# A two-layer graph network in fp32: the set-up's first norm split between two engines, and the output weight transposed earlier

## The chip, the core and the metric

The program runs on one core of a Trainium2 chip. A core has a matrix engine (TensorE; PE in the profile, with its weight loads shown apart as PEld), VectorE (DVE), ScalarE (ACT), GpSimd (POOL) and SyncE (SP), which here only issues transfers. Each engine works through its own queue of instructions in order and waits on semaphores for the others. TensorE reads from the on-chip memory SBUF and writes to PSUM; VectorE and ScalarE take results out of PSUM. Sixteen DMA engines move data between the chip's main memory and SBUF.

The metric is the device time of one execution in microseconds. The median of four runs of the kernel before is 3507.7 us (3506.65 to 3508.15).

## The reference, cut to what matters

The input x is 8 batches of 2048 tokens with 256 features, in fp32, and adj is a 2048 x 2048 adjacency matrix of integers. Each of two layers normalises its input, clamps it at zero, and adds the layer's result to x:

```
h = max(layernorm(x), 0)
x = x + L0(h, adj)          # attention with 4 heads of 64
h = max(layernorm(x), 0)
x = x + L1(h, adj)          # graph attention, one head
```

L0 is this, for each batch, with keys taken in chunks of 256 and a softmax within each chunk:

```
q, k, v = h @ Wq.T + bq, h @ Wk.T + bk, h @ Wv.T + bv
scores  = clip(q . k / 8, -10, 10);  scores = -10 where adj == 0
ctx     = sum over chunks of softmax(scores) @ v
out     = layernorm(ctx @ Wo.T + bo + h) * gamma + beta
```

The four weights Wq, Wk, Wv and Wo are 256 x 256 and enter transposed. L1 projects with another 256 x 256 matrix, builds attention weights from a source term and a target term, masks them by adj, and multiplies.

## The kernel before, in words

**Tiling.** Tokens are handled in blocks of 512 (four tiles of 128), four blocks to a batch. A block's normalised features `hn` (tokens on partitions) are transposed on TensorE into `hT` (features on partitions), from which queries, keys and values are projected. All matmuls are fp32.

**Stages.** A set-up of about 75 us transposes the weights, projects queries, keys and values of all four blocks of batch 0, and turns most of the adjacency matrix into an int8 tile `bound`. Then the batches follow each other. Each has 32 attention steps (`Attention.begin` and `Attention.end`, half a step each), into which other pieces are woven by a table of half-steps: `todo` in general, and `once` (L1153) for pieces that only batch 0 has. Between the attention of two batches stands the second layer.

**Order.** The whole order is written out by hand (`tc.manual_schedule`, L1029): each engine runs its instructions in the order of the source text. A transfer is issued by the queue of the engine that is named, nearly always `nc.sync`, in source order too.

**PSUM.** There are eight banks in three tags of two buffers: `s` (two banks each), `n` and `t`. During set-up `ps_m()` gives `n` and `t` in turn, so that every fourth call reuses a buffer and has to wait until that buffer was emptied; `ps_h()` takes `s`.

**The start of the set-up (L1036 to L1088).** SP issues the loads of block 0's x, of Wq, Wk and Wv (`load_weight`, L233), of three biases, of block 1's x, and of four pieces of adjacency (`load_rows`, L262). Meanwhile TensorE transposes the identity 16 times (`warm(16)`, L1054), which nobody reads. `stats`, `power` and `shift` (L402 to L411) compute block 0's mean and inverse deviation, `stats` and `shift` on VectorE, `power` as three small activations on ScalarE. `turn_weight` (L249) transposes one weight as four 128 x 128 squares into one PSUM tile and copies it out on VectorE; it is called for q, k and v, and eight more identity transposes follow. `norm` (L413, by `normed`, L374) has ScalarE normalise and clamp the four tiles of the block, `Relu(scale * x + bias)`, in two calls. `turn` (L416) transposes a half of the features, and VectorE copies half 0 into `hT`, ScalarE half 1. Then block 1's `stats`, `power` and `shift` are queued, two adjacency pieces are compared with zero (`find`, L1069, by `missing_of`, L271, on VectorE with a copy on GpSimd), and `qk` (L440) projects the queries and then the keys of block 0, each in two PSUM tiles of tag `s`, which ScalarE empties (L451).

**Buffers.** Raw weights and `hn` tiles share one tag of five buffers (`hn_tile`, L210). A tile is one [128, 2, 256] square, so a block takes two.

**The output weight.** It is loaded by `load_output_weight` (L238) as four transfers, because its columns are regrouped by head (runs of 32 values). That happens in half-step 1 of batch 0, after the set-up, and `turn_weight` on it in half-step 5. It is first used in half-step 24 (`output_tiled`, L726, eight half-steps into the second block).

Of the kernel before, what the change touches and what calls it, by code (L numbers as in the profile page):

```python
# [12 lines left out]
AF = mybir.ActivationFunctionType  # L13
ALU = mybir.AluOpType
# [14 lines left out]
def gnn_two_layers(  # L29
# [18 lines left out]
    nc = tc.nc  # L48
# [31 lines left out]
    def ps_m():  # L80
        if turn_about[0]:
            turn_about[1] += 1
            if turn_about[1] % 2:
                return ps_n()
        return ps_t()
# [20 lines left out]
    wqT = const.tile([P, FC, F], F32, name="wqT")  # L106
    wkT = const.tile([P, FC, F], F32, name="wkT")
    wvT = const.tile([P, FC, F], F32, name="wvT")
    woT = const.tile([P, FC, F], F32, name="woT")
# [56 lines left out]
    def in_key_order(queries):  # L166
        return queries.rearrange("p (t i b) -> p t i b", i=QUADS, b=Q)
# [13 lines left out]
    def store_bounds(part):  # L181
        nc.sync.dma_start(of_half(part), bounds[part])
# [16 lines left out]
    def column(src, name):  # L199
        t = const.tile([P, FC], F32, name=name)  # L200
        nc.sync.dma_start(t, src.rearrange("(c p) -> p c", p=P))
        return t
# [7 lines left out]
    def hn_tile(name="hn"):  # L210
        return work.tile([P, 2, F], F32, tag="hn", name=name, bufs=5)
# [6 lines left out]
    def pe(piece):  # L218

        piece.kind = "pe"  # L220
        return piece
# [11 lines left out]
    def load_weight(w):  # L233
        raw = hn_tile("raw")
        nc.sync.dma_start(raw, w.rearrange("(c p) f -> p c f", p=P))
        return raw

    def load_output_weight(w):  # L238

        raw = hn_tile("raw")  # L240
        for c in range(FC):
            of_heads = w[c * P:(c + 1) * P, :].rearrange("p (h k d) -> p h k d", h=HEADS, k=2)
            for k in range(2):
                nc.sync.dma_start(
                    raw[:, c, k * P:(k + 1) * P].rearrange("p (h d) -> p h d", h=HEADS), of_heads[:, :, k, :]
                )
        return raw

    def turn_weight(raw, wT):  # L249
        pt = ps_m()  # L250
        for di in range(FC):
            for do in range(FC):
                k = di * FC + do
                nc.tensor.transpose(pt[:, k * P:(k + 1) * P], raw[:, do, di * P:(di + 1) * P], ident)
        nc.vector.tensor_copy(wT.rearrange("p c f -> p (c f)"), pt)

    HALF = N // 2
    in_setup = [True]
# [106 lines left out]
    def norm_shift(engine, mv, rn):  # L365

        engine.tensor_tensor(rn[:, 1, :], rn[:, 1, :], mv[:, :, 0], op=ALU.mult)  # L367
# [16 lines left out]
    def transposed(hns, c):  # L384

        pt = ps_m()
        for t in range(TB):
            nc.tensor.transpose(pt[:, t * P:(t + 1) * P], hns[t // 2][:, t % 2, c * P:(c + 1) * P], ident)
        return pt


    class Projection:
# [16 lines left out]

        def shift(self, nb):  # L410
            norm_shift(self.adder, self.mv[nb], self.rn[nb])  # L411

        def norm(self, nb, t2):  # L413
            self.hns.setdefault(nb, []).append(normed(self.x[nb], self.rn[nb], t2))
# [621 lines left out]
    proj = Projection(0)  # L1036
    turn_about[0] = True
    raws = {}
    proj.load(0)
    for name, w in (("q", wq), ("k", wk), ("v", wv)):  # L1040
        raws[name] = load_weight(w)
    bq_c = column(bq, "bq_c")
    bk_c = column(bk, "bk_c")
    bv_r = row_bcast(bv, "bv_r")
# [4 lines left out]
    def warm(times):  # L1049
        pt = ps_m()  # L1050
        for k in range(times):
            nc.tensor.transpose(pt[:, k % TB * P:(k % TB + 1) * P], ident, ident)

    warm(16)  # L1054
    proj.stats(0, range(TB))
    proj.power(0)
    turn_weight(raws["q"], wqT)
    proj.shift(0)
    turn_weight(raws["k"], wkT)
    turn_weight(raws["v"], wvT)  # L1060
    warm(8)
    proj.norm(0, 0)
    proj.norm(0, 1)
    proj.load(2)
    proj.turn(0, 0)
    proj.turn(0, 1)
    proj.tiles()

    def find(*parts):  # L1069
# [18 lines left out]
    for nb in range(NNB - 1):  # L1088
        i = 6 * nb
# [52 lines left out]
    def layer1_vector(i):  # L1142
        a_r = work.tile([P, F], F32, tag="r", name="a_r")
        nc.sync.dma_start(a_r, row(a1[i * F:(i + 1) * F, 0]))
        prod = hn_tile("prod")
        for c in range(FC):
            nc.vector.scalar_tensor_tensor(
                prod[:, c, :], w1s[:, c, 0:F], 1.0, a_r, op0=ALU.mult, op1=ALU.mult,
                accum_out=w1s[:, c, F + i:F + i + 1],
            )  # L1150


    once = {  # L1153
        1: [lambda: raws.update(o=load_output_weight(wo)), layer1_weight],
        2: [lambda: [store_bounds(part) for part in HALVES_OF[:3]]],
        5: [pe(lambda: turn_weight(raws["o"], woT))],
        6: [lambda: layer1_vector(0)],
        7: [lambda: layer1_vector(1)],
        HALVES - PER: [find_lone],
# [305 lines left out]
```

## Time and profile before

| what | value |
|---|---|
| median of four runs | 3507.7 us |
| profiled execution | 3507.57 us |
| its span, first to last instruction | 3505.8 us |
| TensorE busy | 3496.7 us (100%) |
| VectorE, ScalarE, GpSimd busy | 75%, 56%, 52% |
| granted TensorE clock | 1.00 |
| DMA in the first fortieth of the span (88 us) | 247 GB/s, engines 70 to 80% busy |

A row of the timeline has the start in us, the duration in us, the engine, the line of the kernel, the operation, what it writes and reads (out<-in), the shape and how often it ran; in brackets stands the idle time of the engine before it and what ended it. SPq is the sequencer of SP issuing transfers. The chain that ended last is read backwards by the profiler from the last instruction, at each step to what released it; its rows have start, duration and the work. Matmul ends are modelled, so that a busy TensorE is not one at its peak.

### The profile page before, as it was taken

The page shows a single profiled execution, that of the slowest core. Times are in us where ns is not written, and L with a number is a line of the kernel's source. Part 1 is how long each engine was busy: PE and PEld are TensorE (multiplying, and loading weights), DVE is VectorE, ACT ScalarE, POOL GpSimd, SP SyncE. Part 2 cuts the span into 40 slices and gives each one's busy share as a digit, 9 for nine tenths or more (in the row PEclk, how much of TensorE's full clock was granted, in tenths as well). Part 3 has the DMA queues.
Part 4 walks back from the last instruction along what each step waited for, and adds up shares of the span by engine and source line. Part 5 has one row for each costly group of instructions (what it writes and reads, how often), then busy time and mean ns, then how long its engine had stood idle before and what let it go on. Part 6 is the DMA issues. An engine that isn't in the chain of part 4 may idle for free.

```text
span 3505.8 us, 104599 instructions
## 1 busy us (share of the span) xinstructions
PE 3496.7 (100%) x46076; PEld 2308.5 (66%) x46076; DVE 2632.3 (75%) x3983; ACT 1958.3 (56%) x2961; POOL 1824.6 (52%) x1198
## 2 busy tenths in 40 slices
PE   9999999999999999999999999999999999999999
PEld 5455775667765577566876758656686655864578
DVE  6887777877678676786767867678686785857876
ACT  6777426763267633676336763367623776147751
POOL 5677017870278702786037850378503784047841
PEclk9999999999999999999999999999999999999999
DMA  7545323443234531444314443244432335124331
GB/s 247 127 109 124 95 87 72 97 111 105 67 87 86 119 100 61 92 93 110 103 61 92 93 106 103 65 92 87 121 103 65 79 85 128 62 53 93 80 79 52
DMA packets 171320, 332.13 MB, mean 95 GB/s; under 512 B 28656, under 2 KB 90352, under 8 KB 170864
## 3 DMA queue, kind: packets, MB, share of 16 engines
q0 software_dynamic: 32832, 119.03, 18.6%
q1 hardware_dynamic: 129712, 205.36, 18.3%
q8 instruction: 360, 5.90, 0.7%
q10 hardware_dynamic: 8320, 1.05, 0.2%
q14 instruction: 96, 0.79, 0.1%
HBM read 156.50 MB, written 51.44 MB: 59 GB/s over the span
## 4 chain that ended last, share of the span: by engine, by line
PE 98%; DVE 1%; ACT 0%; DMA 0%; POOL 0%; issue 0%; ACTq 0%; DVEq 0%; POOLq 0%
PE ps_s L503 25%; PE ps_n L519 25%; PE ps_s L994 12%; PE ps_t L531 7%; PE ps_n L994 6%; PE ps_t L994 6%; PE ps_t L743 2%; PE ps_t L447 2%; PE ps_n L447 2%; PE ps_s L447 2%; PE ps_n L461 2%; PE ps_t L843 1%; PE ps_t L461 1%; PE ps_n L843 1%; PE ps_s L843 0%; PE ps_n L721 0%
## 5 line engine op out<-in xcount | busy, mean ns | idle before, releaser
L543 DVE SCALAR_TENSOR_TENSOR e<-ps_s,bound 128x1024 f32<-128x1024 f32 x1024 | 1219.0, 1221 | 400.4 <-PE ps_s L503 395.4
L558 POOL TENSOR_TENSOR both<-e 128x1024 f32<-128x1024 f32 x512 | 1221.7, 2417 | 542.4 <-PE ps_t L531 245.2
L503 PE MATMUL ps_s<-q,k 64*32 64x512 f32 x16384 | 1332.3, 590 | 0.1
L552 ACT ACTIVATE e<-e 128x1024 f32<-128x1024 f32 x1024 | 1049.1, 1049 | 456.2 <-DVE e L543 439.0
L519 PE MATMUL ps_n<-e,v 64*32 64x512 f32 x16384 | 1118.3, 589 | 0.0
L503 PEld LDWEIGHTS ps_s<-q,k 64*32 64x32 f32 x16384 | 504.3, 106 | 399.2 <-issue 277.9
L519 PEld LDWEIGHTS ps_n<-e,v 64*32 64x32 f32 x16384 | 523.8, 107 | 361.8 <-issue 266.5
L531 PE MATMUL ps_t<-both,ones 64*32 64x512 f32 x4096 | 548.1, 590 | 0.0
L994 PE MATMUL ps_s<-g,w 128*128 128x257 f32 x2048 | 448.5, 380 | 0.0
L994 PEld LDWEIGHTS ps_s<-g,w 128*128 128x128 f32 x2048 | 388.7, 190 | 55.7
L573 DVE TENSOR_TENSOR prod<-ps_n,rz 128x512 f32<-128x512 f32 x448 | 288.9, 687 | 135.9 <-ACT rz L564 86.5
L1017 POOL TENSOR_TENSOR x<-x,r 128x256 f32<-128x256 f32 x124 | 90.5, 744 | 457.1 <-ACT r L1015 456.3
L977 DVE SCALAR_TENSOR_TENSOR w<-bound,w 128x1024 f32<-128x1024 int8 x256 | 314.7, 1229 | 8.7
L367 POOL TENSOR_TENSOR krn<-krn,mv 128x4 f32<-128x4 f32 x28 | 6.7, 240 | 560.9 <-DVE w L971 560.9
L994 PE MATMUL ps_n<-g,w 128*128 128x257 f32 x1024 | 292.5, 382 | 0.0
L994 PE MATMUL ps_t<-g,w 128*128 128x257 f32 x1024 | 289.9, 380 | 0.0
L563 ACT ACTIVATE rz<-ps_t 128x512 f32<-128x512 f32 x256 | 152.4, 595 | 237.5 <-PE ps_t L531 164.2
L971 DVE TENSOR_SCALAR w<-src,cd 128x512 f32<-128x512 f32 x512 | 263.4, 557 | 17.7 <-ACT src L951 13.8
L578 POOL DMA_DIRECT2D ctxT<-prod x224 | 192.6, 860 | 56.5 <-DVE sd L852 50.2
L994 PEld LDWEIGHTS ps_n<-g,w 128*128 128x128 f32 x1024 | 193.0, 190 | 44.1 <-issue 17.6
L531 PEld LDWEIGHTS ps_t<-both,ones 64*32 64x32 f32 x4096 | 151.7, 106 | 101.9 <-SPq L475 44.1
L994 PEld LDWEIGHTS ps_t<-g,w 128*128 128x128 f32 x1024 | 194.0, 189 | 28.0
(139 smaller groups left out, 2974.0 us busy)
## 6 DMA issues: line engine op xcount, KB each, us to landing
ctxT<-prod POOLq DMA_DIRECT2D x224, 512.0 KB, 5.0
bound<-bound_d SPq DMA_DIRECT2D x125, 512.0 KB, 4.5
turned_d<-squares SPq DMA_DIRECT2D x232, 128.0 KB, 2.8
hT<-turned_d SPq DMA_DIRECT2D x58, 512.0 KB, 4.6
rows<-in_adj_dram SPq DMA_DIRECT2D x32, 512.0 KB, 5.0
x<-in_x_dram SPq DMA_DIRECT2D x32, 512.0 KB, 6.3
out_dram<-x SPq DMA_DIRECT2D x31, 512.0 KB, 2.7
xp<-in_x_dram SPq DMA_DIRECT2D x28, 512.0 KB, 4.5
```

Source lines behind the costliest of these rows:

```text
L447: nc.tensor.matmul(in_key_order(pp) if i == 0 else pp, w[:, di, do * P:(do + 1) * P], h, start=di == 0, stop=di == FC - 1,)
L503: nc.tensor.matmul(self.s[n, o][c * Q:(c + 1) * Q, kt, :], self.k[p][rows, at:at + Q], self.q[p][rows, nb * NB:(nb + 1) * NB], start=True, ...
L519: made.append(nc.tensor.matmul(self.num[n, c][h * Q:(h + 1) * Q, :], self.v[rows, j * KT + kt, at:at + Q], self.e[n, p][rows, i * KT + kt, :],
L531: nc.tensor.matmul(self.total[n][h * Q:(h + 1) * Q, :], ones[rows, :], self.both[n, h // 2][rows, h % 2, :], start=half == 1, stop=half == 0,)
L543: nc.vector.scalar_tensor_tensor(self.e[n, p][:, i * KT:(i + 1) * KT, :], self.s.pop((n, o)), -CLIP * SC, bounds[nb, j // 4][:, j % 4 * KT ...
L552: nc.scalar.activation(e, e, AF.Exp, scale=1.0 / SC)
L558: nc.gpsimd.tensor_tensor(self.both[n, p], e[:, 0], e[:, 1], op=ALU.add)
L573: nc.vector.tensor_tensor(dst[:, c, :], self.num.pop((n, c)), self.rz[n], op=ALU.mult)
L578: nc.gpsimd.dma_start(self.ctxT[nb], self.prod.pop(n), accum_op=ALU.add)
L971: nc.vector.tensor_scalar(w[:, i, :], self.src[nb], self.cd[:, 0, j:j + 1], self.cd[:, 1, j:j + 1], op0=ALU.mult, op1=ALU.max,)
L977: nc.vector.scalar_tensor_tensor(two, bounds1[nb, j // 8][:, j % 8 - 1:j % 8 + 1, :], 0.0, two, op0=ALU.is_gt, op1=ALU.mult)
L994: nc.tensor.matmul(accs[t][:, 0:F + 1], w[:, i, t * P:(t + 1) * P], g[:, j, :], start=j == 0, stop=j == NT - 1,)
```

## The change

Five edits, all in the set-up or in what it takes over from the loop:

1. The four loads of the output weight are issued right after those of Wq, Wk and Wv, ahead of the biases, of block 1's x and of the adjacency.
2. Its transposes stand behind those of q, k and v, in the place of the eight identity transposes. In the loop, half-steps 1 and 5 lose the load and the transposes.
3. Transposing a weight and taking it out of PSUM are two calls now. The copy of q stays where it was. That of k goes to ScalarE, behind its norms; those of v and o stay on VectorE and come behind the eviction of the block's first half.
4. Two of the block's four tiles are normalised by VectorE, without the clamp.
5. Both evictions of the transposed block clamp at zero, VectorE with a maximum, ScalarE with Relu. For the two tiles that ScalarE clamped already this changes nothing.

```
-    def turn_weight(raw, wT):
+    def turned_weight(raw):
         pt = ps_m()
...
-        nc.vector.tensor_copy(wT.rearrange("p c f -> p (c f)"), pt)
+        return pt
+
+    def keep_weight(pt, wT, engine):
+        dst = wT.rearrange("p c f -> p (c f)")
+        if engine is nc.vector:
+            nc.vector.tensor_copy(dst, pt)
+        else:
+            nc.scalar.activation(dst, pt, AF.Copy)
...
+        def norm_signed(self, nb, t2):
+            hn, rn = hn_tile(), self.rn[nb]
+            for i in range(2):
+                t = 2 * t2 + i
+                nc.vector.tensor_scalar(
+                    hn[:, i, :], self.x[nb][:, t, :], rn[:, 0, t:t + 1], rn[:, 1, t:t + 1], op0=ALU.mult, op1=ALU.add
+                )
+            self.hns.setdefault(nb, []).append(hn)
+
+        def turn_signed(self, nb, c):
+            if c == 0:
+                self.hT[nb] = Features()
+            pt = in_key_order(transposed(self.hns[nb], c))
+            if c == 0:
+                nc.vector.tensor_scalar(self.hT[nb].queries(0), pt, 0.0, None, op0=ALU.max)
+            else:
+                nc.scalar.activation(self.hT[nb].queries(c), pt, AF.Relu)
...
         raws[name] = load_weight(w)
+    raws["o"] = load_output_weight(wo)
...
-    turn_weight(raws["q"], wqT)
+    keep_weight(turned_weight(raws["q"]), wqT, nc.vector)
     proj.shift(0)
-    turn_weight(raws["k"], wkT)
-    turn_weight(raws["v"], wvT)
-    warm(8)
+    turned = {name: turned_weight(raws[name]) for name in "kvo"}
     proj.norm(0, 0)
-    proj.norm(0, 1)
+    proj.norm_signed(0, 1)
+    keep_weight(turned["k"], wkT, nc.scalar)
     proj.load(2)
-    proj.turn(0, 0)
-    proj.turn(0, 1)
+    proj.turn_signed(0, 0)
+    keep_weight(turned["v"], wvT, nc.vector)
+    keep_weight(turned["o"], woT, nc.vector)
+    proj.turn_signed(0, 1)
     proj.tiles()
...
-        1: [lambda: raws.update(o=load_output_weight(wo)), layer1_weight],
+        1: [layer1_weight],
...
-        5: [pe(lambda: turn_weight(raws["o"], woT))],
```

## The prediction

> **What bounds the kernel now.** I read the page first, for the whole span.
>
> ```profile
> PE 3496.7 (100%) x46076; PEld 2308.5 (66%) x46076; DVE 2632.3 (75%) x3983; ACT 1958.3 (56%) x2961; POOL 1824.6 (52%) x1198
> ...
> PE 98%; DVE 1%; ACT 0%; DMA 0%; POOL 0%; issue 0%; ACTq 0%; DVEq 0%; POOLq 0%
> ```
>
> TensorE is busy all the time, and the chain that ended last runs 98% through it. So a microsecond is won or lost only where TensorE starts earlier, has less to do, or idles. The change touches the first 16 us and one spot near 80 us; I took the chain of waits there in order of time.
>
> ```profile
> 7.98 2.08 ACT hn L379 x4
> 10.11 0.34 PE ps_t L388
> 10.47 0.70 DVE hT L421
> 11.21 7.21 PE ps_s L447 x16
> ...
> 79.95 0.59 PE ps_t L254 x4
> 80.53 0.56 PE ps_t L531 x4
> ```
>
> Four norms in a row on ScalarE, then transposes, the eviction, and from 11.21 TensorE without a break. The chain shows one path only; whether a second lies close behind is in the timeline, engine by engine.
>
> ```profile
> 4.20 0.43 SPq L207 DMA_DIRECT2D both<-in_x_dram  x1
> ...
> 7.98 2.07 ACT L379 ACTIVATE hn<-both,krn 128x256 f32<-128x256 f32 x4 [0.23 <-DVE krn L367]
> 8.46 0.68 DVE L255 COPY wvT<-ps_t 128x512 f32<-128x512 f32 x1
> 10.47 0.69 DVE L421 COPY hT<-ps_t 128x512 f32<-128x512 f32 x1 [1.33 <-PE ps_t L388]
> 11.08 0.42 DVE L356 BATCH_NORM_STATS2 stats<-both 128x6 f32<-128x256 f32 x1
> 13.33 0.30 ACT L361 ACTIVATE krn<-mv,eps 128x4 f32<-128x4 f32 x1 [1.83 <-DVE mv L357]
> 14.01 0.67 ACT L451 ACTIVATE q<-ps_s,bq_c 128x512 f32<-128x512 f32 x1
> 14.73 0.30 PEld L447 LDWEIGHTS ps_s<-hT,wkT 128*128 128x128 f32 x2 [0.64 <-ACT q L451]
> 14.75 3.67 PE L447 MATMUL ps_s<-hT,wkT 128*128 128x512 f32 x8
> ...
> 56.34 3.69 SPq L244 DMA_DIRECT2D raw<-in_L_gnn_Wo_dram  x4
> ...
> 80.57 0.69 DVE L255 COPY woT<-ps_t 128x512 f32<-128x512 f32 x1 [1.87 <-PE ps_t L254]
> 81.18 2.35 DVE L543 SCALAR_TENSOR_TENSOR e<-ps_s,bound 128x1024 f32<-128x1024 f32 x2
> 83.58 0.15 PEld L503 LDWEIGHTS ps_s<-q,k 64*32 64x32 f32 x12 [0.39 <-DVE e L543]
> ```
>
> There is a second path. The key matmuls at 14.75 need the PSUM buffer that ScalarE's first query eviction (14.01) frees. That eviction is queued behind the three small activations of block 1's power (from 13.33), which wait for VectorE's statistics of block 1 (from 11.08), which are queued behind the hT eviction (10.47). The key weights were ready to load at 14.73 and TensorE went on at 14.75, so the two paths end together.
>
> **Part by part: the first query matmul.** Shift ends at 7.94. ScalarE now does two of the four norms; the 2.07 for four are about 0.49 apart, so the second ends near 9.06. VectorE does the other two from about 7.9: by L1147 (same 128x256, 0.42) or half of L971 (TENSOR_SCALAR, 541 ns median for 512 columns, so 0.27) they end between 8.5 and 8.8, inside ScalarE's two; cost nothing while that cover stands. The Trainium skill, "VectorE: DVE Perf Modes", section on the perf-mode tier table, gives fp32 tensor_scalar from SBUF twice the single rate. Row L971 runs at the single rate; by the page these two norms would end some 0.25 sooner, and the sum would be the same.
>
> TensorE's order is now q, k, v, o, then the block's transposes. Loads for q, k, v landed at 5.38, 6.53 and 7.23, when their transposes started. Wo's four DMAs are issued from 2.67. In the row at 56.34 they hold SP's queue for 3.69, and the DMA view narrowed to each gives 4.9, 4.5, 4.7 and 3.1 us to landing; the last lands 62.5, about 1.5 behind the rows load in front (61.06 by the same view). Taken 1.5 behind Wv, that is 8.7; taken as 3.1 after an issue at 5.7, it is 8.8. I take 8.8. The o transposes (0.42 for four, row L254) then end near 9.2, just when the second norm is done; the block's four follow, the last at about 9.35, and 0.36 later (10.11 to 10.47 in the chain) VectorE clamps: **9.7 instead of 10.47**. The clamp reads the same PSUM tile as the copy, so I price it as the copy (0.69; L466, also from PSUM, is 0.69 too). First query matmul: 9.7 + 0.74 = **10.45 instead of 11.21**. The second transposes need the PSUM buffer of k, which ScalarE now empties behind its norms (as L423, 0.60: free at 9.65), so its Relu ends near 11.0; the third matmul needs it at 11.3. Nothing waits.
>
> **Part by part: the key matmuls.** The copies of v and o now stand on VectorE between the clamp and the statistics of block 1: 0.60 each from start to start (7.86 to 8.46). Statistics start at 9.7 + 0.61 + 0.60 + 0.60 = 11.5 instead of 11.08. They also need block 1's x. Its load moves on SP behind Wo's four and three small loads: from 4.20 to between 7.2 (Wv landed: the rows loads at 5.36, 6.51 and 7.21 went out just after Wq, Wk and Wv landed, eight DMAs back, so SP seems to hold eight in flight) and 7.9 (3.69 + 3 x 0.51 behind 2.67). The first x took 3.9 to land on an empty queue, so 11.1 to 11.8. I take 11.6 for the start. The rest follows rigidly: 11.08 to 14.75 was 3.67, so keys start at **15.25 instead of 14.75: a loss of 0.5**, and the 0.76 won at the queries ends as TensorE idling. From 14.75 TensorE is dense up to a 0.47 wait at 50.94, and the engines around it wait on it, so I carry the 0.5 through. Bounds: 0.3 (the second norm at 9.06 keeps the clamp from starting before about 9.55) to 2.0 (x landing 5.7 after 7.9, as it did in a full queue, is 13.6: statistics 2.5 late, less slack in the chain at 50).
>
> The four rows loads go out from about 8.4 and land from about 13 at 1.3 apart (before, by the DMA view, 11.2 to 15.0); their finds now start near 14.7 and are 1.15 apart, so the last (needed after 18) keeps a microsecond. x of block 2 is issued near 9.5 instead of 10.08 (its buffer is free when the norms are), behind them: no cost. POOL's queue gets nothing new, but its first z copy waits for the finds and shifts with them.
>
> **The loop.** Out come four transposes (0.59 in the chain) and a 0.69 copy ahead of two clips. The weights at 83.58 waited 0.39 for such a clip, so without the copy's end moving too the 0.59 would not hold; it moves (0.60), so both go. At most also half the array's lag there (83.06 to 83.58), 0.5; at least nothing, if the clips set the pace. I take **-0.7**. On SP, w1s, three bound stores and two rows loads go out up to 3.7 earlier, into DMA engines 86 to 100% busy between 55 and 70, less Wo's own traffic: ScalarE's 2.07 wait at 71.21 for a bound_part store shortens, but TensorE is dense from 70.30 to 79.8 and gains nothing; bounds -0.4 (its idle before 70.30) to +0.4 (a bound_part store pushed later).
>
> **Clock.** Eight warm transposes (7.73 to 8.77) go, and TensorE may idle from 7.9 to about 8.5. The first 16 weight loads took 3.27 (0.20 each), the eight later ones 0.90 (0.11), so the array ran at half speed until about 6.5, though the granted clock reads 1.00 there. It kept full speed over the idle 10.87 to 11.21 between two sparse stretches; I take no cost. The Trainium skill, "TensorE: Matmul & The Clock Gate", Part 4, says transposes do not count as activity for the clock, which this trace contradicts, since only transposes ran before it sped up. Its Part 1 wants some 3.4 us idle before the clock drops; by that the gap costs nothing, and the sum is the same.
>
> **Sum.** +0.5 - 0.7 = -0.2 on a span of 3505.8: 3505.6. The profiled execution took 3507.57, 1.77 more than its span, and the median of the four runs is 3507.7, 0.13 above it. So 3505.6 + 1.77 + 0.13 = **3507.5**.
>
> **Rivals.** *The gain goes through:* if the query eviction does not wait for block 1's power, keys start 0.76 early; with 0.7 and the bound 0.5 of the loop that is 3507.7 - 2.0 = 3505.7. For it: the chain shows only the norm path. Against: 13.33 to 14.73 are queued on one engine without a gap. *Wo comes late and blocks TensorE (slower):* the o transposes stand in front of the block's own, so past a landing at about 8.9 each microsecond of Wo delays the clamp, the statistics and the keys by as much. It decides the sign from 9.0 on (0.2 late). At 11.3 (the 4.9 us of its slowest piece after an issue at 6.4) it is 2.4 later, -0.2 + 2.4: 3509.9. Against: 3.1 for the last piece, measured in a busy queue. *The clock falls back:* eight query matmuls at 0.86 instead of 0.43 cost 3.4, of which the idle before the keys (about 1.4) hides part: +2.0, 3509.5. *The statistics wait for x:* its 2.0 instead of 0.5 gives 3509.0.
>
> **How the numbers follow.** Forecast 50%, its own range 3506.5 to 3508.3 (0.3 to 0.9 in setup, -1.2 to 0 in the loop). Gain through 13%; Wo late 14%; x late 12%; clock 5%; something unseen 6%. The range from 3505.3 to 3509.7 leaves out about 2 in 10, the late ends of Wo and x among it. 0.2% is 7.0 us, about what a measurement of this kernel can tell from no change; no case here reaches it, so faster 2%, same 95%, slower 3%, the rest being what I do not see.
>
> **What would show it.** Right: clamp near 9.7, first query matmul near 10.45, a TensorE gap of about 1.3 before the keys, which start near 15.25 behind the query eviction; sums (L531 of before) directly behind the logits near 79.7, no copy of woT there. Wrong: keys before 14.75; the o transposes after 9.0; warm-speed rows (0.11 per load) back at 0.20; or the 0.5 of setup swallowed by the wait at 50.94, if the stores that end it do not shift with TensorE.

## The result: 5.2 us slower, and the profile after

| | before | after |
|---|---|---|
| median of all runs | 3507.64 us (60 runs, 3506.63 to 3511.37) | 3512.87 us (42 runs, 3510.50 to 3514.43) |
| ratio | | 1.0014, 95% interval 1.0010 to 1.0019 |
| profiled execution | 3507.57 us | 3512.14 us |
| its span | 3505.8 us | 3510.4 us |

The change costs 5.2 us by the medians and 4.6 us between the two profiled executions. That is within 0.2%, as forecast, but above the range of the prediction (3505.3 to 3509.7). The page of the kernel after looks as before at first, TensorE busy and the chain on it:

```profile
PE 3497.2 (100%) x46068; PEld 2360.6 (67%) x46068; DVE 2630.5 (75%) x3984; ACT 1958.0 (56%) x2960; POOL 1824.8 (52%) x1198
...
PE 98%; DVE 1%; ACT 0%; DMA 0%; POOL 0%; SPq 0%; issue 0%; ACTq 0%; DVEq 0%; POOLq 0%
```

One word is new, SPq: SyncE's issuing of transfers has come into the chain. The chain of the first 24 us, in order of time (start, duration, work), shows where:

```profile
2.68 0.65 SPq L244
...
5.39 1.09 SPq L201
...
7.55 6.32 DMA both<-in_x_dram
13.88 0.44 DVE stats L363
...
17.55 5.40 PE ps_s L472 x8
22.94 0.89 PE ps_z L303 x16
```

Before, this chain ran from the load of block 0's x over its norm to the queries. Now the norm is not in it. It goes from SyncE issuing the four pieces of Wo (L244) and the biases (L201, L196) to block 1's x (`both`), which is issued at 7.55 and lands at 13.86, and from there over block 1's statistics, ScalarE's power and the query eviction to the keys. The timeline has the same with the waits in brackets:

```profile
9.59 0.69 DVE L434 TENSOR_SCALAR hT<-ps_t 128x512 f32<-128x512 f32 x1 [0.99 <-PE ps_t L395]
...
10.34 3.70 PE L472 MATMUL ps_s<-hT,wqT 128*128 128x512 f32 x8 [0.19 <-DVE hT L434]
...
13.88 0.43 DVE L363 BATCH_NORM_STATS2 stats<-both 128x6 f32<-128x256 f32 x1 [2.41 <-DMA both<-in_x_dram]
...
17.55 5.40 PE L472 MATMUL ps_s<-hT,wkT 128*128 128x512 f32 x8 [3.51 <-ACT q L476]
```

The first query matmul is 0.87 us earlier than before (10.34 against 11.21). But VectorE, done with the copies of the weights at 11.47, stands 2.41 us until x lands, and the keys start 2.80 us later than before (17.55 against 14.75), behind 3.51 us in which TensorE has nothing to do. A second loss follows: the same eight key matmuls take 5.40 us where they took 3.67, and the next step on TensorE (22.94) is 4.51 late. The table of one-microsecond windows says why (columns: window, its length, then the busy share of PE, PEld, DVE, ACT and POOL with their instructions, the granted clock, the busy share of the DMA engines, GB/s):

```profile
18.00:19.00 1.00, 1.00 (x3) 0.38 (x2) 1.00 (x3) 1.00 (x4) 0.68 (x1) 0.92 0.63 254
19.00:20.00 1.00, 1.00 (x3) 0.45 (x2) 1.00 (x3) 1.00 (x3) 0.98 (x2) 0.50 0.73 164
...
22.00:23.00 1.00, 1.00 (x6) 0.32 (x5) 0.93 (x5) 0.02 (x1) 0.84 (x1) 0.88 0.88 291
```

The clock column falls to half speed at about 18.84 and is back at about 22.24; the two windows left out read 0.50 as well. The missing parts, 0.08 + 3 x 0.50 + 0.12, add up to 1.70 us; the difference between 2.80 and 4.51 is 1.71.

Now the 6.3 us that x took. The windows in which it waited, first of the kernel after:

```profile
7.00:8.00 1.00, 1.00 (x8) 0.71 (x7) 0.77 (x3) 0.71 (x4) 0.00 (x0) 1.00 0.32 24
8.00:9.00 1.00, 0.46 (x3) 0.14 (x1) 0.60 (x2) 1.00 (x3) 0.00 (x0) 1.00 0.48 63
9.00:10.00 1.00, 0.99 (x7) 0.73 (x7) 0.41 (x1) 0.43 (x1) 0.00 (x0) 1.00 0.53 31
```

and of the kernel before:

```profile
7.00:8.00 1.00, 0.96 (x9) 0.77 (x8) 0.81 (x3) 0.71 (x4) 0.00 (x0) 1.00 0.88 227
8.00:9.00 1.00, 0.96 (x8) 0.66 (x6) 1.00 (x2) 1.00 (x3) 0.00 (x0) 1.00 1.00 398
```

Before, the DMA engines moved 227 and 398 GB/s in the first two of these microseconds (410 in the third). After, they moved 24 to 63: SyncE had spent 2.68 to 7.0 on issues with few bytes in them, and the engines ran dry. The view of transfers (name, queue, size, issue to landing) shows what stood ahead of x:

```profile
both<-in_x_dram SPq DMA_DIRECT2D x1, 512.0 KB, 6.3
...
bv_r<-in_L_gnn_bv_dram SPq DMA_DIRECT2D x1, 128.0 KB, 5.5
```

`bv_r` is one bias row of 1 KB read once for each of the 128 partitions (`row_bcast`, L196). It was issued at 7.04 and landed at 12.55, and x, issued next, landed 1.3 us behind it. Before it was the same pair in a full queue, `bv_r` from 3.69 and x from 4.20, which again landed 1.3 behind it, at 9.9:

```profile
both<-in_x_dram SPq DMA_DIRECT2D x1, 512.0 KB, 5.7
bv_r<-in_L_gnn_bv_dram SPq DMA_DIRECT2D x1, 128.0 KB, 4.9
```

VectorE got to it only at 11.08, so x came 1.2 us early and its long way did not show. In all eight traces here in which `bv_r` stands just ahead of x, x lands 6.2 to 6.4 us after the issue of `bv_r` where the DMA engines have work, and 6.8 to 6.9 where they run dry. So of the 4.0 us by which x lands late, 3.35 are the later issue of `bv_r`, and only some 0.6 come with the dry engines.

Further on, TensorE's wait in front of the values, which the prediction named at 50.94, did not shrink. By the view of waits (who waits, for whom, us in total, times, longest) it is 0.8 us after and was 0.5 before, in both behind ScalarE's work on `bound_part`. After:

```profile
PE ps_n L486 <- ACT bound_part L321: 0.8, 1, 0.8
```

and before:

```profile
PE ps_n L461 <- ACT bound_part L314: 0.5, 1, 0.5
```

So the first clip of the attention (near 56 us) is 4.82 us late. In half-step 5 the transposes and the copy of the output weight are gone, the sums follow the logits directly, and the shift falls by 1.0, to 3.81:

```profile
83.50 1.14 PE L528 MATMUL ps_s<-q,k 64*32 64x512 f32 x16
...
84.36 0.61 PE L556 MATMUL ps_t<-both,ones 64*32 64x512 f32 x4
```

Some 0.8 comes back later in batch 0, of which 0.45 near 285 us and 0.35 by 366. From there on it stays at +4.6. The one place of this that a trace names is a weight load of the sums that waits for SyncE's queue, after:

```profile
287.79 0.13 PEld L556 LDWEIGHTS ps_t<-both,ones 64*32 64x32 f32 x5 [0.88 <-SPq L500]
```

and before:

```profile
283.38 0.13 PEld L531 LDWEIGHTS ps_t<-both,ones 64*32 64x32 f32 x5 [0.29 <-SPq L475]
```

L500 (L475 before) is an empty instruction on SyncE that keeps two matmul groups on one PSUM bank in order (`fence`). It stands behind the fetch of a bound tile, which took 0.64 us to issue instead of 0.37, and the weight loads behind it waited 0.88 instead of 0.29.

The sum by the traces: keys +2.80, clock +1.70, the wait near 50 +0.3, half-step 5 -1.0, given back +0.8: **+4.6**, the difference of the spans.

### The profile page after: what moved, and what is told of

Read it like the earlier page. It is cut to its first block, busy times and chain, and to the rows that moved or that the text cites. A ratio compares the mean times of both kernels' runs of the same rounds, so it can differ in the third digit from the quotient of the medians.

```text
span 3510.4 us, 104583 instructions
## 1 busy us (share of the span) xinstructions
PE 3497.2 (100%) x46068; PEld 2360.6 (67%) x46068; DVE 2630.5 (75%) x3984; ACT 1958.0 (56%) x2960; POOL 1824.8 (52%) x1198
## 4 chain that ended last, share of the span: by engine, by line
PE 98%; DVE 1%; ACT 0%; DMA 0%; POOL 0%; SPq 0%; issue 0%; ACTq 0%; DVEq 0%; POOLq 0%
PE ps_s L528 25%; PE ps_n L544 25%; PE ps_s L1019 12%; PE ps_t L556 6%; PE ps_n L1019 6%; PE ps_t L1019 6%; PE ps_t L768 2%; PE ps_n L472 2%; PE ps_t L472 2%; PE ps_s L472 2%; PE ps_n L486 2%; PE ps_t L486 1%; PE ps_t L868 1%; PE ps_n L868 1%; PE ps_s L868 0%; PE ps_n L746 0%
## 5 line engine op out<-in xcount | busy, mean ns | idle before, releaser
L528 PEld LDWEIGHTS ps_s<-q,k 64*32 64x32 f32 x16384 | 524.3, 106 | 384.9 <-issue 248.6
L544 PEld LDWEIGHTS ps_n<-e,v 64*32 64x32 f32 x16384 | 555.0, 107 | 329.4 <-issue 204.8
```

Of the source, the lines that this page charges most:

```text
L528: nc.tensor.matmul(self.s[n, o][c * Q:(c + 1) * Q, kt, :], self.k[p][rows, at:at + Q], self.q[p][rows, nb * NB:(nb + 1) * NB], start=True, ...
L544: made.append(nc.tensor.matmul(self.num[n, c][h * Q:(h + 1) * Q, :], self.v[rows, j * KT + kt, at:at + Q], self.e[n, p][rows, i * KT + kt, :],
```

## Experiments

The theory from these traces: Wo's early load makes block 1's x late, the late x makes TensorE idle, and the idle time makes the clock fall. Rivals: VectorE's new order (the copies of v and o ahead of the statistics) or the split norm itself costs the time; the 256 KB of Wo cost it by their size, and not the way in which they are issued. Shifts "at the first clip" and "at the end" are read by comparing the same instructions in the traces of the run and of the kernel before.

### Wo's load early, nothing else

The kernel before, with Wo's load at the new place; it lands in `woT` itself, which is free until the transposes in half-step 5.

```
-        raw = hn_tile("raw")
+        raw = woT
...
+    raws["o"] = load_output_weight(wo)
     bq_c = column(bq, "bq_c")
...
-        1: [lambda: raws.update(o=load_output_weight(wo)), layer1_weight],
+        1: [layer1_weight],
```

> The kernel before with one part of the change: the output weight's four loads are issued behind Wv, ahead of the biases and of block 1's x (they land in woT itself, where the transposes of half-step 5 read them and the copy overwrites them). Theory 'late x': block 1's x lands near 13.9 instead of 9.9, its statistics wait for it, the key matmuls start near 17.5 instead of 14.75 and, after 3.5 us of idle TensorE, take 5.4 instead of 3.7; the loop keeps its transposes. 4.5 to 4.8 slower than before: 3512.3. Rival 'VectorE order' (the moved copies hold the statistics): nothing of that is here, so 3507.6 within 0.5.

Measured: 3511.81 us (11 runs, 3510.29 to 3513.11) against 3507.54 on the same chip; ratio 1.0012 (1.0003 to 1.0020). Its timeline:

```profile
14.24 0.43 DVE L356 BATCH_NORM_STATS2 stats<-both 128x6 f32<-128x256 f32 x1 [3.35 <-DMA both<-in_x_dram]
...
17.91 3.70 PE L447 MATMUL ps_s<-hT,wkT 128*128 128x512 f32 x8 [3.26 <-ACT q L451]
```

The load alone has most of the loss: x lands at 14.22 and the keys start 3.2 us late. In this profiled run (3511.00 us) they ran at full speed, 3.70. The eleven times lie in two groups, and the mean clock of each run parts them in the same way: five from 3510.29 to 3511.00 with a mean of 1.000, six from 3511.81 to 3513.11 with 0.999. A stretch of 3.4 us at half speed is 0.0005 of the mean, so the two groups can be the clock not falling and falling. The rounded mean alone does not decide it for one execution: the profiled one of the kernel after has such a stretch and still reads 1.000, as 11 of its 42 do.

### Everything but Wo

The kernel after, with Wo loaded, transposed and copied where it was before, and the eight identity transposes back.

```
-    raws["o"] = load_output_weight(wo)
...
-    turned = {name: turned_weight(raws[name]) for name in "kvo"}
+    turned = {name: turned_weight(raws[name]) for name in "kv"}
+    warm(8)
...
-    keep_weight(turned["o"], woT, nc.vector)
...
-        1: [layer1_weight],
+        1: [lambda: raws.update(o=load_output_weight(wo)), layer1_weight],
...
+        5: [pe(lambda: keep_weight(turned_weight(raws["o"]), woT, nc.vector))],
```

> The change without the output weight: norm split, clamp behind the transposes, k copied by ScalarE and v behind the clamp, the eight identity transposes kept, Wo loaded and transposed in the loop as before. Theory 'late x': x lands near 9.9 as before, the clamp starts near 9.6, statistics near 10.8, keys near 14.5 (0.25 sooner than before): 3507.3, between 3506.9 and 3507.9. Rival 'VectorE order': 2 to 4 slower than before, 3509.6 to 3511.6.

Measured: 3507.55 us against 3507.54; ratio 1.0000 (0.9991 to 1.0009). From its timeline:

```profile
14.60 3.70 PE L472 MATMUL ps_s<-hT,wkT 128*128 128x512 f32 x8 [0.41 <-ACT q L476]
```

With v's copy alone ahead of them, the statistics start at 10.95 and the keys at 14.60, against 11.08 and 14.75 before. The rival of the split norm and of VectorE's order falls: that half of the change moves the median by 0.01 us. The copy of o is not in it; with both copies, in the run with `bv_r` behind the adjacency further on, the keys start at 15.04, 0.3 later than before. The queries start 0.7 us earlier (10.49), and all of it ends in a wait, as the second path said.

### Block 1's x ahead of Wo

The kernel after, with x of block 1 issued ahead of Wo.

```
+    proj.load(1)
     raws["o"] = load_output_weight(wo)
     bq_c = column(bq, "bq_c")
     bk_c = column(bk, "bk_c")
     bv_r = row_bcast(bv, "bv_r")
-    proj.load(1)
```

> The whole change, with block 1's x issued behind Wv, ahead of the output weight and the biases. Theory 'late x': x lands before 9, Wo near 9.5, statistics near 11.8, keys between 15.1 and 15.6 at full speed (0.4 to 0.8 late), 1.0 won in the loop and up to 0.8 of it lost again: 3506.9 to 3508.2. Rival 'warm transposes' (the clock falls because the eight identity transposes are gone): keys at half speed still, 3509.5 or more.

Measured: 3509.06 us (3507.78 to 3510.61) against 3507.54; ratio 1.0004 (0.9996 to 1.0013). Better than the kernel after by 3.8, and still above what I expected. The timeline:

```profile
9.14 0.30 PE L254 MATMUL ps_n<-ident,raw 128*128 128x128 f32 x1 [0.95 <-DMA raw<-in_L_gnn_Wo_dram]
...
16.23 3.70 PE L472 MATMUL ps_s<-hT,wkT 128*128 128x512 f32 x8 [1.01 <-ACT q L476]
```

Now x lands at 8.78, but Wo only at 9.92. Its transposes stand in front of the block's own on TensorE, the clamp slips to 10.77, the statistics behind it to 12.57, and the keys to 16.23. This is the prediction's rival "Wo comes late and blocks TensorE", here with its price: o transposes ending 2.2 us later than in the kernel after, clamp 1.2 later. The order of these two loads is no way out: one of them is late either way. In this profiled execution the keys ran at full speed, but six of the eleven have a mean clock of 0.999 (3508.60 to 3510.61 us, the other five 3507.78 to 3509.41). So the clock fell in those too; where it did is not shown, and no wait of the profiled one comes near 3 us. The missing eight transposes alone do not make it fall: the run with `bv_r` behind the adjacency has none of them either, and all eleven of its executions read 1.000.

### Filling the idle time of TensorE

The kernel after with 32 transposes of the identity between queries and keys, which nobody reads.

```
         if nb == 0:
+            warm(16)
+            warm(16)
             proj.norm(1, 0)
```

> The whole change, with 32 identity transposes (3.5 us) between the query and the key matmuls of block 0, where TensorE otherwise idles. Theory 'late x' with the clock as its second half: keys start near 17.55 as in the changed kernel and take 3.7 instead of 5.4, so 1.7 less than the changed kernel: 3511.1. If the clock has no part: 3512.8, unchanged.

Measured: 3510.24 us (3509.47 to 3511.41), 2.6 below the kernel after; ratio to before 1.0008 (1.0000 to 1.0017). The timeline:

```profile
13.70 1.91 PE L1078 MATMUL ps_t<-ident 128*128 128x128 f32 x16
...
17.45 3.70 PE L472 MATMUL ps_s<-hT,wkT 128*128 128x512 f32 x8
```

The keys start where they did (17.45, x landed at 13.76), and take 3.70 instead of 5.40. So work that does nothing saves time: it takes away the clock's loss and leaves that of the late x. All eleven runs have a mean clock of 1.000, against 11 of 42 of the kernel after. Between the profiled executions it is worth 1.9 us, by the medians 2.6; why the median of the kernel after lies 0.7 above its own profiled execution is not settled.

### `bv_r` behind the adjacency

The kernel after, with the load of `bv_r` moved behind the four adjacency pieces. It is not read before the values.

```
     bk_c = column(bk, "bk_c")
-    bv_r = row_bcast(bv, "bv_r")
     proj.load(1)
...
     rows = {i: load_rows(*nearest[i]) for i in range(4)}
+    bv_r = row_bcast(bv, "bv_r")
```

> The whole change, with the broadcast load of the values' bias (bv_r) issued behind the four adjacency loads instead of ahead of block 1's x. In every profile so far bv_r lands 5 us or more after its issue and block 1's x lands 1.3 behind it. Theory 'bias ahead': without it x lands near 11.0, statistics start near 11.4 (VectorE's copies), keys near 15.1 at full speed (0.3 late), 1.0 won in the loop, up to 0.8 of it lost again: 3506.8 to 3507.9. Rival 'small pieces' (the output weight's short runs hold up the DMA engines): x lands near 13.4 as before, keys near 17 and time 3510 or more.

Measured: 3507.21 us (3506.18 to 3508.72) against 3507.63; ratio 0.9999 (0.9990 to 1.0007). One small load moved, and 5.7 us are back. The keys in its timeline:

```profile
15.04 3.70 PE L472 MATMUL ps_s<-hT,wkT 128*128 128x512 f32 x8 [1.06 <-ACT q L476]
```

x was issued at 7.35, at nearly the time of the kernel after (7.55), and landed 4.0 us later, at 11.35; in the kernel after it was 6.3 us later. By the windows the engines were as dry at first (58 and 63 GB/s from 7 to 9), and then filled:

```profile
9.00:10.00 1.00, 1.00 (x7) 0.67 (x7) 0.47 (x1) 0.37 (x1) 0.00 (x0) 1.00 0.91 344
```

This window is the difference, 344 GB/s against 31. The view of transfers has the row:

```profile
both<-in_x_dram SPq DMA_DIRECT2D x1, 512.0 KB, 4.0
```

This is also the schedule that the prediction described: statistics at 11.38 (forecast 11.5), keys at 15.04 (15.25), a gap of 1.06 (1.3), time 3507.2 (3507.5). The time agrees in part by luck: the profiled execution is 0.3 slower than that of before, 0.55 late at the first clip and only 0.25 better over the loop, where 0.7 was forecast.

### The same, and the first query eviction ahead of block 1's power

As above, and ScalarE empties the first PSUM tile of queries before the three small activations that wait for block 1's statistics.

```
     proj.stats(1, range(TB))
+    proj.qk(0, 0, ps_h, halves=[0])
     proj.power(1)
...
-        proj.qk(nb, 0, ps_h)
+        proj.qk(nb, 0, ps_h, halves=range(FC) if nb else [1])
```

> As the run with bv_r behind the rows, and the first half of block 0's query eviction stands ahead of block 1's power on ScalarE. If the queue on ScalarE is what holds the keys, they start near 14.0 (0.75 sooner than before) and the time falls to 3506.0 to 3507.0; if something else does, they stay near 15.1: 3506.8 to 3507.9.

Measured: 3506.22 us against 3507.63; ratio 0.9996 (0.9987 to 1.0005, which takes in no change). But ten of its eleven runs lie between 3505.68 and 3506.50, below the lowest of the 33 runs of the kernel before beside it (3507.03); the eleventh is 3508.18. The timeline:

```profile
13.39 0.30 ACT L368 ACTIVATE krn<-mv,eps 128x4 f32<-128x4 f32 x1 [0.60 <-DVE mv L364]
13.62 3.60 PE L472 MATMUL ps_s<-hT,wkT 128*128 128x512 f32 x8
```

The keys start at 13.62, behind the queries without a gap. The shift against before is -0.87 at the first clip, the 0.87 of the first query matmul: with the order on ScalarE mended, the earlier norm counts in full. At the end it is -1.3.

### The loop's part alone

The kernel before, with Wo loaded near 30 us into `woT` and transposed in the set-up near 70 us, between two pieces of `bound`.

```
-        raw = hn_tile("raw")
+        raw = woT
...
             beta_r = row_bcast(beta, "beta_r")
+            raws["o"] = load_output_weight(wo)
...
-    bound(22, 23)
+    bound(22)
+    turn_weight(raws["o"], woT)
+    bound(23)
...
-        5: [pe(lambda: turn_weight(raws["o"], woT))],
```

> The kernel before with only the loop's part of the change: the output weight is loaded behind beta near 30 us (into woT itself) and transposed near 70 us, where TensorE idles 0.4; the loop loses the load and the transposes, the first 28 us stay as they are. 0.6 to 1.0 less at half-step 5; if SyncE's queue takes back as much as in the changed kernel near 285 us, 0.2 of it stays: 3506.6 to 3507.5.

Measured: 3507.17 us (3506.68 to 3509.81) against 3507.63; ratio 0.9999 (0.9990 to 1.0008). In the trace -0.23 at the first clip, -0.47 after half-step 5, and -0.15 to -0.30 from 288 us on. The medians do not tell this gain from noise; in the trace it is there, but smaller than in the kernel after, and part of it goes back at the same fence (a wait of 0.60 there).

### Wo early and `bv_r` late, on the kernel before

The first experiment with `bv_r` behind the adjacency.

```
+    raws["o"] = load_output_weight(wo)
     bq_c = column(bq, "bq_c")
     bk_c = column(bk, "bk_c")
-    bv_r = row_bcast(bv, "bv_r")
...
     rows = {i: load_rows(*nearest[i]) for i in range(4)}
+    bv_r = row_bcast(bv, "bv_r")
```

> The run with only the output weight's load moved, and bv_r behind the four adjacency loads besides. Theory 'bias ahead': x lands near 11, statistics near 11.1, keys between 14.7 and 15.0, and the 4 us of that run are gone: 3507.4 to 3508.0. Rival 'small pieces': x near 13.5, 3510.5 or more.

Measured: 3507.65 us against 3507.63; ratio 1.0000 (0.9992 to 1.0009). From its timeline:

```profile
11.07 0.43 DVE L356 BATCH_NORM_STATS2 stats<-both 128x6 f32<-128x256 f32 x1 [0.22 <-DMA both<-in_x_dram]
```

x was issued at 7.20 instead of 4.20 and landed at 11.05, in time for the statistics (11.08 before). So the 3.0 us by which SyncE comes late to x cost nothing by themselves, by the medians; they cost 4.2 us with `bv_r` between them and x.

### Wo early with the idle time filled

The first experiment with the 32 identity transposes between queries and keys.

```
         if nb == 0:
+            warm(16)
+            warm(16)
             proj.norm(1, 0)
```

> The run with only the output weight's load moved, with 32 identity transposes between block 0's query and key matmuls. That run's executions lie in two groups about 2 us apart (3510.3 to 3511.0 and 3511.8 to 3513.1), and its profiled one, of the lower group, had the keys at full speed after 3.26 us of idle TensorE. If the upper group is executions in which the clock fell, keeping TensorE busy leaves the lower group alone: all between 3510.2 and 3511.2, median 3510.7. If the groups have another cause they stay, median 3511.8.

Measured: 3510.99 us against 3507.68; ratio 1.0010 (1.0001 to 1.0019). All eleven runs lie in one group, 3510.65 to 3511.75, all with a mean clock of 1.000. The upper group of the first experiment is gone, which agrees with the clock falling in some executions and not in others. The lower group is not beaten: here the transposes end behind the eviction and the keys start at 18.30.

### Wo in one plain load

The kernel after with Wo loaded as the other three weights are, 256 KB in one transfer. The regrouping of its columns by head is left out, so this kernel multiplies by a weight whose columns are in the wrong order.

```
-    raws["o"] = load_output_weight(wo)
+    raws["o"] = load_weight(wo)
```

> The whole change, with the output weight loaded by one plain transfer of the same 256 KB, without the regrouping of its columns by head (so the attention's output projection mixes the wrong columns). If it is the four issues of short runs that let the DMA engines run dry in front of bv_r and x, SyncE reaches x near 4.7 and x lands near 10.6: statistics near 11.4, keys near 15.1, 3506.8 to 3507.9. If it is the 256 KB as such, or bv_r alone, x lands near 13.5 and the time stays at 3512 to 3513.

Measured: 3507.37 us (3506.63 to 3508.32) against 3507.68; ratio 0.9999 (0.9990 to 1.0008). One window of its trace:

```profile
7.00:8.00 1.00, 0.97 (x10) 0.74 (x7) 0.77 (x3) 0.71 (x4) 0.00 (x0) 1.00 0.83 192
```

The bytes are the same and the order too, `bv_r` ahead of x. But x is issued at 4.72, the engines have work (192 GB/s here against 24), `bv_r`'s 5.1 us lie beside other transfers, and x lands at 10.55, 6.3 us after the issue of `bv_r` at 4.21, as in the kernel before. The rival of the 256 KB falls. It is the late issue behind four pieces of short runs that costs, together with `bv_r`; without either of them the loss is gone.

## Why the prediction was wrong, by its steps

**Right: the first path.** Clamp at 9.59 (forecast 9.7), first query matmul at 10.34 (10.45), o transposes at 7.35 to 8.1. Wo's pieces landed between 7.1 and 7.7, earlier than the 8.8 that I took, so the rival "Wo comes late" did not come about in this kernel; the third experiment shows that it was a real one. So the clamp came out near the forecast for another reason: ScalarE's second norm held it (until 8.95), which the prediction had as its bound of 9.55. VectorE's two norms took 0.74 together, within the 0.54 to 0.84 that the forecast allowed. Its remark that row L971 runs at a single rate is not settled: 0.41 us for 256 columns here and 0.54 for the 512 of that row differ by only 0.13.

**Right: the second path.** The keys hang on the chain from VectorE's statistics over ScalarE's power to the query eviction, and the gain of the norm ends there in a wait. Without Wo, that part of the change is worth 0.0 us. When the eviction is taken out of that queue, the 0.87 goes through.

**Wrong: the landing of x, "The first x took 3.9 to land on an empty queue, so 11.1 to 11.8".** The issue was right (7.55, forecast 7.2 to 7.9), though by luck in its parts: the issues of Wo took 2.67 where 3.69 was forecast, and that of the first bias 1.09 instead of 0.51. The queue was empty, but `bv_r` stood in front. I had listed it among "three small loads" and counted the time of its issue, not of its landing. Measured: `bv_r` 5.5 us, x 1.3 behind it, landing at 13.86. The trace of before held the row for it: `bv_r` 4.9 us and x 1.3 behind. By my own times for SyncE `bv_r` goes out one issue (0.5) ahead of x, at 6.7 to 7.4; with 4.9 + 1.3 behind that, x lands at 12.9 to 13.6. With `bv_r` out of the way x took 4.0, and the prediction's schedule and time came out.

**Wrong in size: the rival of the late x, 2.0.** It had x at 13.6, 0.26 from the measured value, and took 2.5 less some slack near 50 us. The slack was not there: the wait at 50.94 is 0.8 instead of 0.5, and the stores that end it shifted with TensorE. The late x cost 2.80 + 0.3.

**Wrong: "Clock ... I take no cost".** I had looked for the clock at the short gap from 7.9 to 8.5 and priced it as a rival of its own, with an idle time of 1.4 before the keys. But the clock depends on the late x: x late means 3.51 us idle, and that brought 1.70 more. Two rivals with 12% and 5% were one case, and their common price, 2.80 + 1.70 against 0.5, lay outside the range. (The forecast's own range has a slip besides: 0.3 to 0.9 and -1.2 to 0 around 3507.7 give 3506.8 to 3508.6, not 3506.5 to 3508.3. It changes nothing here.) That there are two losses is shown: filling the idle time removes the one and leaves the other. The Trainium skill, "TensorE: Matmul & The Clock Gate", Part 1, puts the fall of the clock after one or more idle windows of some 3.4 us, with windows that run freely. The half-speed stretch of 3.4 us, a gap of 3.51 with a fall and one of 3.26 without, and runs that lie in two groups agree with that in size. But the 3.4 us just before the fall at 18.84 were not idle: TensorE worked in the last 1.3 of them. What exactly makes the clock fall stays open.

**Right in sign, with a give-back: the loop.** Forecast -0.7 (-1.2 to 0); measured -1.0 at half-step 5. Of it 0.45 is lost again near 285 us and 0.35 by 366. The first place is the fence behind the bound fetch: that issue took 0.37, 0.35, 0.64 and 0.96 us in the traces of before, of the loop's part alone, of after and of the fastest kernel, and the wait behind it was 0.29, 0.60, 0.88 and 0.90. The issue alone does not explain the wait: the loop's part alone waits 0.60 with an issue of 0.35. Why either is longer stays open.

## What to carry to other kernels

When a load is moved ahead of others, go through every transfer behind it by its own time from issue to landing in the trace, and not by the time of its issue. A slow small load (here `bv_r`) holds up the one behind it whether the engines are busy or dry; before, it did not show because it was issued early enough. A load that is not needed yet (here a bias row for all partitions) belongs behind the ones that are. And when TensorE would idle for as long as here (3.51 us in the profiled execution with a fall, 3.26 in the kernel of which six of eleven executions read a lower clock), price the clock together with the wait, as one case.

## What the hardware showed that I had not expected

- A read of one 1 KB row for 128 partitions (128 KB) takes 5.5 us from issue to landing with the DMA engines half idle, longer than a 512 KB load of x (4.0); it is 4.9 to 5.6 in all nine traces in which it goes out ahead of the adjacency, with the engines busy or not. Why is open.
- In the kernel after, SyncE took 0.62 to 0.65 us for the issue of a 64 KB piece in short runs and 1.09 for the 1 KB column of a bias behind them (0.47 before, 2.73 in the run with x ahead of Wo), and 0.44 for 512 KB of x. This moved the issue of x from 4.20 to 7.55; with the same bytes in one plain load it is 4.72.
- The clock fell 1.3 us after TensorE had gone back to work (18.84 against 17.55), so the gap looks harmless at its end, and the loss is seen only in the duration of later matmuls and in the clock column.
- Transposes alone keep TensorE at full speed: 32 of them in the gap, and the keys took 3.70 and 3.60 us. The Trainium skill, "TensorE: Matmul & The Clock Gate", Part 4, says that transposes in TensorE's transpose mode do not count as busy for the clock in the same way; if the fp32 transposes here run in that mode, which no trace shows, these two runs contradict it.
